# A two-layer graph attention network on one core: layer 1's edge masks made by ScalarE in two operations instead of by one comparison on VectorE

## Chip, cores and metric

The kernel runs on one core of a Trainium2 chip. The metric is the device time of one execution in microseconds (us). Three runs of the kernel before took 2610.62, 2584.36 and 2599.78 us, so the median is 2599.78 us. The other two lie 0.4 and 0.6% from it.

## What is computed

The input is a graph of N = 6250 nodes with 768 features and E = 100000 edges, sorted by destination node. The node features go through a layer norm and a ReLU, then two graph attention layers, then a two-layer perceptron, and the result is added to the input:

```python
h = jnp.maximum(_layernorm(x, axis=-1), 0.0)
x = x + _L0_gnn_ref(h, edge_index, W1, ..., bm2)

def gat_conv(x, src, dst, W, a_src, a_dst, bias, heads):
    h = (x @ W).reshape(n, heads, -1)
    alpha_s = (h * a_src[None]).sum(-1)
    alpha_d = (h * a_dst[None]).sum(-1)
    e = jax.nn.leaky_relu(alpha_s[src] + alpha_d[dst], NEG_SLOPE)
    m = jax.ops.segment_max(e, dst, num_segments=n)
    e = jnp.exp(e - m[dst])
    denom = jax.ops.segment_sum(e, dst, num_segments=n)
    alpha = e / (denom[dst] + 1e-16)
    out = jax.ops.segment_sum(h[src] * alpha[:, :, None], dst, num_segments=n)
    return out.reshape(n, -1) + bias
```

Each node also has an edge to itself. Layer 1 has 4 heads of 64 features, layer 2 one head of 256. The work that matters here is the edge work of layer 1: for each edge, fetch the source node's row, find the weight of the edge from a number of the source and a number of the destination, and add the weighted row to the destination's sum.

## The kernel before

**Tiling.** Nodes are in 49 tiles of 128 (NT). Edges are in tiles of 128; four edge tiles make a group g (196 groups), two groups make a unit u (98 units), and four groups g = 4t to 4t+3 make a period t, which belongs to node tile t because the edges are sorted by destination. The stages follow each other: features of layer 1 (until about 190 us), edges of layer 1 (about 195 to 1420 us), edges of layer 2 with the perceptron (about 1480 us to the end).

**One group of layer 1.** GpSimd (POOL) issues one indirect DMA for each edge tile, which gathers the source rows from the table in DRAM into `G` (line 700), up to 8 groups ahead. VectorE (DVE) compares the destinations with a row of numbers 0 to 127 to make the one-hot matrices `hot` (line 724). It works out the edge weights in lines 781 and 782, multiplies the gathered rows with them into `hw` (line 784), and TensorE (PE) adds them up per destination with `o_ps += hot^T hw` (line 804). VectorE takes finished sums over into `acc` (line 822), ScalarE (ACT) copies their parts into `sum` (line 831).

**The masks.** To give every edge the factor of its destination node, the kernel needs the transposed one-hot matrix, `mask`: the row of destinations (mod 128) of 1024 edges is loaded into all 128 partitions (`drow`, bf16, line 660 on the SP queue), and partition p of the mask is 1 where the destination equals p. One VectorE operation makes the mask of a unit, 128x1024 bf16, in `make_mask` (line 714), with the partition's number p (`pidx_ps`) as second operand. TensorE then multiplies the 16 edge tiles of a period with a table of node factors into `e_parts` (line 747, function `meet`); ScalarE copies the result out as `parts_sb` (line 759, `parts_out`), and VectorE adds its three parts up (line 766, `join`). `parts` has one PSUM buffer, so the next `meet` waits for `parts_sb`. In the loop over g, `make_mask` is called at g = 4t+1 and g = 4t+3 for the `meet` at the start of period t+1, whose factors are used in period t+3. There are 98 masks, six buffers for masks and three for `drow`.

**Finished nodes.** When a tile of sums is complete, a generator (`Node1.steps`) is advanced twice per group and turns it into a row block of layer 2: VectorE lines 1050 to 1068, TensorE transposes into `tp` (line 1010), ScalarE `rT` (line 1016), TensorE `h_ps` (line 1076), ScalarE `kept` and `sd` (lines 1080, 220, 221, 1084), and a store into layer 2's table on the SP queue.

**Missing rows.** 46 gathers of layer 1 were issued before the table was complete. What they lack is added later: VectorE makes `soon_hit` (line 335), TensorE multiplies it with the rows kept on chip (`missing`, line 346, 2 to 20 node tiles each), and VectorE adds the product to `G` (line 353). VectorE executes in order, so behind line 353 stand the weights and `hw` of the same group.

**Order of the work.** The kernel gives every engine its instructions in the order of the Python code; there is no scheduler that would move them. An instruction waits for semaphores of the engines or DMAs whose results it needs, and everything behind it on its engine waits with it.

Of the kernel before, what the change touches and what calls it, by code (L numbers as in the profile page):

```python
# [10 lines left out]
F32 = mybir.dt.float32  # L11
BF16 = mybir.dt.bfloat16
I32 = mybir.dt.int32
AF = mybir.ActivationFunctionType
ALU = mybir.AluOpType
AX = mybir.AxisListType

P = 128
# [9 lines left out]
NT = -(-N // P)  # L28
# [44 lines left out]
def kernel(  # L73
# [21 lines left out]
    nc = tc.nc  # L95
# [3 lines left out]
    def pool(name, bufs, **kw):  # L99
        return ctx.enter_context(tc.tile_pool(name=name, bufs=bufs, **kw))  # L100

    const = pool("const", 1)
# [15 lines left out]
    pidx = const.tile([P, 1], F32, name="pidx")  # L118
# [9 lines left out]
    late_nid = min(SOON_FROM, NEXT_FROM)  # L128
    wide = 4 * (HID // 4 + 1)
# [3 lines left out]
    def part_ps(n):  # L133
        at_ps[0] += n
        return both_ps[:, at_ps[0] - n:at_ps[0]]

    iota_ps, nid_ps, mine_ps, rden_ps, pidx_ps = (part_ps(n) for n in (P, NT - late_nid, wide, 8, 1))
    own_ps = part_ps(4 * P - at_ps[0])
    nc.vector.tensor_copy(iota_ps, iota)
    nc.vector.tensor_copy(nid_ps, nid[:, late_nid:])  # L140
    nc.vector.tensor_copy(pidx_ps, pidx)
    eps_c = const.tile([P, 1], F32, name="eps_c")
    nc.vector.memset(eps_c, EPS)
    idle = const.tile([P, 4 * P], BF16, name="idle")
# [1 line left out]
    ones_c = const.tile([P, 1], F32, name="ones_c")  # L146
# [499 lines left out]
    drow, mask = {}, {}  # L646
# [15 lines left out]
    def layer_edges(layer, H, node, pre, matched, pre_pool):  # L662
# [4 lines left out]
        with tc.tile_pool(name=f"eg{layer}", bufs=6) as eg, \  # L667
# [36 lines left out]
            def both(u):  # L704
                return tiles(2 * u)[0], TPG + tiles(2 * u + 1)[-1] + 1

            def make_mask(u):

                if layer == 2 or not 0 <= u < NU:
                    return  # L710
                a, b = (t * P for t in both(u))
                mask[u] = maskp.tile([P, 8 * P], BF16, name="mask")
                at = u % 2 * 8 * P
                nc.vector.tensor_tensor(mask[u][:, a:b], drow[u // 2][:, at + a:at + b],  # L714
                                        pidx_ps.to_broadcast([P, b - a]), ALU.is_equal)

            def make_hot(g):

# [150 lines left out]
            if layer == 1:  # L869
                fetch_rows(0)  # L870
                soon_away(0)
                for r in range(1, 3):
                    fetch_rows(r)
                soon_sources(pre_pool, 0)
                fetch_rows(3)
                for u in range(4):
                    make_mask(u)
            else:
                next_away()
# [55 lines left out]
            for g in range(NG):  # L935
# [20 lines left out]
                if j == 0:  # L956
                    if layer == 1:
                        fetch_rows(t + 4)
                    node.prefetch(t)
                    if layer == 1:  # L960
                        meet(t + 2 if t > 0 else 1)
                elif j == (2 if t < NT - 1 else 1):
                    node.ahead(t)
                elif j % 2 and (layer == 2 or t > 0):
                    make_mask((g + (11 if layer == 1 else 7)) // 2)
                if layer == 1 and t == 0:
                    for u in ((), (4, 5), (6,), (7,))[j]:
                        make_mask(u)
                    if j == 1:
                        parts_out(1)  # L970
                    if j == 2:
                        meet(2)
# [576 lines left out]
```

## Time and profile before

| what | value |
|---|---|
| median of three runs | 2599.78 us |
| the profiled execution: time, span | 2625.26 us, 2623.5 us |
| mean granted TensorE clock in it | 0.809 of full speed |
| busy: PE, DVE, ACT, POOL | 1760.9, 1544.5, 426.2, 1522.5 us |
| the 98 masks (line 714) on VectorE | 118.1 us together |

The page lists the busy time of each engine, then the span in 40 slices, the DMA queues, the chain of work that ended last, and the costliest groups of instructions with the idle time of their engine just before them and what ended it. `PEld` is the weight load of a matmul. Starts of matmuls are recorded, but their ends are modelled, so an engine that waits for a matmul may start well after the end that is shown. A releaser that the profile could not name is "remote" in the lists of waits and "another core or an unknown queue" in the chain; with one core it is not another core.

### The profile page before, as it was taken

The page shows a single profiled execution, that of the slowest core. Times are in us where ns is not written, and L with a number is a line of the kernel's source. Part 1 is how long each engine was busy: PE and PEld are TensorE (multiplying, and loading weights), DVE is VectorE, ACT ScalarE, POOL GpSimd, SP SyncE. Part 2 cuts the span into 40 slices and gives each one's busy share as a digit, 9 for nine tenths or more (in the row PEclk, how much of TensorE's full clock was granted, in tenths as well). Part 3 has the DMA queues.
Part 4 walks back from the last instruction along what each step waited for, and adds up shares of the span by engine and source line. Part 5 has one row for each costly group of instructions (what it writes and reads, how often), then busy time and mean ns, then how long its engine had stood idle before and what let it go on. Part 6 is the DMA issues. An engine that isn't in the chain of part 4 may idle for free.

```text
span 2623.5 us, 23350 instructions
## 1 busy us (share of the span) xinstructions
PE 1760.9 (67%) x7244; PEld 1321.8 (50%) x7246; DVE 1544.5 (59%) x2880; ACT 426.2 (16%) x1330; POOL 1522.5 (58%) x1666
## 2 busy tenths in 40 slices
PE   9861776767577678677666247777666667666667
PEld 7751555555455456455554135455545455554444
DVE  7633566656655756656656256656556655665565
ACT  6640011111111111111112001111111111111111
POOL 5256655655655655555564656666666666666660
PEclk9985888878788777788777578988788888887789
DMA  9885334444433444444442634444444444444441
GB/s 350 284 252 173 111 107 118 115 114 115 128 114 110 125 118 113 120 114 113 124 111 71 181 81 121 141 118 134 131 123 136 127 128 128 134 133 126 120 130 66
DMA packets 144491, 351.43 MB, mean 134 GB/s; under 512 B 33815, under 2 KB 57454, under 8 KB 144358
## 3 DMA queue, kind: packets, MB, share of 16 engines
q0 software_dynamic: 75040, 210.90, 29.5%
q1 hardware_dynamic: 68092, 137.74, 16.1%
q10 hardware_dynamic: 1226, 1.22, 0.2%
q8 instruction: 59, 0.97, 0.2%
q14 instruction: 74, 0.61, 0.1%
HBM read 308.14 MB, written 41.59 MB: 133 GB/s over the span
## 4 chain that ended last, share of the span: by engine, by line
DVE 30%; PE 27%; another core or an unknown queue 25%; issue 12%; ACT 2%; POOL 2%; DMA 2%; DVEq 1%; SPq 0%; POOLq 0%; ACTq 0%
PE o_ps L804 13%; DVE hot L724 5%; PE missing L346 5%; DVE hw L784 4%; PE h_ps L494 4%; DVE u_ps L797 3%; DVE u_ps L795 3%; DVE mask L714 3%; DVE soon_hit L335 2%; PE y_ps L1204 2%; DVE hot L798 2%; POOL G L700 2%; DVE acc L822 2%; PE missing L404 1%
## 5 line engine op out<-in xcount | busy, mean ns | idle before, releaser
L700 POOL DMA_INDIRECT G<-table,src_i x1498 | 1420.4, 948 | 974.4 <-issue 381.7
L804 PE MATMUL o_ps<-G,hot 128*128 128x258 f32 x1564 | 471.7, 457 | 373.2 <-DVE hot L798 235.9
L804 PE MATMUL o_ps<-hw,hot 128*128 128x260 f32 x1564 | 508.6, 473 | 243.8 <-issue 100.9
L804 PEld LDWEIGHTS o_ps<-G,hot 128*128 128x128 f32 x1564 | 350.6, 230 | 479.8 <-DVE hot L798 258.4
L804 PEld LDWEIGHTS o_ps<-hw,hot 128*128 128x128 f32 x1564 | 354.8, 234 | 356.7 <-issue 128.8
L831 ACT ACTIVATE sum<-acc 32x260 f32<-32x260 f32 (+1 forms) x384 | 160.0, 417 | 1137.3 <-DVE acc L822 549.0
L795 DVE TENSOR_TENSOR u_ps<-rho_ps,G 128x512 f32<-128x512 f32 (+1 forms) x197 | 135.3, 687 | 323.0 <-remote 286.9
L346 PE MATMUL missing<-kept,soon_hit 128*128 128x268 f32 x1028 | 263.6, 407 | 31.0 <-issue 30.2
L724 DVE TENSOR_TENSOR hot<-iota_ps,dcol 128x512 f32<-128x512 f32 x392 | 265.8, 679 | 0.0
L784 DVE TENSOR_TENSOR hw<-G,factors 128x1040 f32<-128x1040 f32 (+1 forms) x198 | 242.2, 1223 | 35.3 <-remote 22.3
L353 DVE SCALAR_TENSOR_TENSOR G<-G,soon_ok,missing 128x268 f32<-128x268 f32 x46 | 22.7, 493 | 385.6 <-remote 219.6
L346 PEld LDWEIGHTS missing<-kept,soon_hit 128*128 128x128 f32 x1028 | 200.7, 198 | 76.8 <-issue 41.2
L1204 PE MATMUL y_ps<-wm,mT 128*128 128x384 f32 x392 | 157.2, 525 | 0.6 <-ACT mT L1199 0.6
L494 PE MATMUL h_ps<-w,r 128*128 128x264 f32 (+1 forms) x588 | 144.1, 400 | 18.2 <-ACT r L484 9.6
L797 DVE TENSOR_TENSOR u_ps<-u_ps,G 128x512 f32<-128x512 f32 (+1 forms) x197 | 136.7, 694 | 6.7
L798 DVE TENSOR_TENSOR hot<-hot,u_ps 128x512 f32<-128x512 f32 (+1 forms) x197 | 134.2, 681 | 6.8
L494 PEld LDWEIGHTS h_ps<-w,r 128*128 128x128 f32 x588 | 112.5, 198 | 40.4 <-ACT r L484 10.5
L714 DVE TENSOR_TENSOR mask<-drow,iota_ps 128x1024 bf16<-128x1024 bf16 x98 | 118.1, 1207 | 13.4 <-DMA drow<-dmod_d 13.4
L1204 PEld LDWEIGHTS y_ps<-wm,mT 128*128 128x128 f32 x392 | 68.2, 194 | 60.9 <-issue 33.7
L311 POOL DMA_INDIRECT G<-table,soon_i x46 | 45.6, 991 | 86.9 <-DMA bT<-in_b 54.3
L1080 ACT ACTIVATE kept<-h_ps 128x256 f32<-128x256 f32 x49 | 18.9, 385 | 461.5 <-remote 334.9
L822 DVE SCALAR_TENSOR_TENSOR acc<-acc,keep,o_ps 128x260 f32<-128x260 f32 (+1 forms) x192 | 91.6, 477 | 1.9 <-PE o_ps L804 1.9
(433 smaller groups left out, 1425.9 us busy)
## 6 DMA issues: line engine op xcount, KB each, us to landing
xt<-in_x SPq DMA_DIRECT2D x96, 384.0 KB
drow<-dmod_d SPq DMA_DIRECT2D x49, 512.0 KB
G<-table,src_i POOLq DMA_INDIRECT x1498
out<-y SPq DMA_DIRECT2D x48, 384.0 KB
xTt<-in_xT SPq DMA_DIRECT2D x41, 384.0 KB
table<-kept SPq DMA_DIRECT2D x49, 134.0 KB
table<-kept SPq DMA_DIRECT2D x49, 129.5 KB
soon_d<-G SPq DMA_DIRECT2D x23, 268.0 KB
```

What stands on the lines that cost most here:

```text
L346: nc.tensor.matmul(soon_p[k], hit[:, T - there], kept[T], start=(T == there), stop=(T == NT - 1))
L494: nc.tensor.matmul(h_ps[:, :n], r[:, k], w1[:, k, :n], start=(k == 0), stop=(k == KI - 1))
L700: nc.gpsimd.indirect_dma_start(out=G[g][:n, t], out_offset=None, in_=table[layer], in_offset=bass.IndirectOffsetOnAxis(ap=src_i[:n, k:k + ...
L714: nc.vector.tensor_tensor(mask[u][:, a:b], drow[u // 2][:, at + a:at + b], pidx_ps.to_broadcast([P, b - a]), ALU.is_equal)
L724: nc.vector.tensor_tensor(hot[g][:, T[0]:T[0] + n], iota_ps.unsqueeze(1).to_broadcast([P, n, P]), dcol[:, k:k + n].unsqueeze(2).to_broadca ...
L784: nc.vector.tensor_mul(hw[:, of], Gg[:, :, :RW[1]].rearrange("p t (h c) -> p t h c", h=H), w.unsqueeze(3).to_broadcast([P, n, H, C + 1]))
L795: nc.vector.tensor_mul(u_ps[:, of], row.unsqueeze(1).to_broadcast([P, n, P]), e2.to_broadcast([P, n, P]))
L797: nc.vector.tensor_max(u_ps[:, of], u_ps[:, of], e1.to_broadcast([P, n, P]))
L798: nc.vector.tensor_mul(hot[g][:, of], hot[g][:, of], u_ps[:, of])
L804: nc.tensor.matmul(o_ps[u], hot[g][:, k], r, start=(g % 2 == 0 and k == 0), stop=(g % 2 == 1 and k == tiles(g)[-1]))
L831: nc.scalar.activation(done[t][r], acc[r], AF.Copy)
L1204: nc.tensor.matmul(y_ps, mT[:, j], wm2[:, j, s * half:(s + 1) * half], start=False, stop=(j == KH - 1))
```

## The change

`make_mask` no longer uses VectorE. ScalarE first writes the absolute difference |d - p| of the destination and the partition's number into the mask (function Abs, with the bias -p from a new constant `less_p`), then overwrites it with max(0, 1 - that) (function Relu, scale -1, bias 1). For whole numbers this is 1 where they are equal and 0 elsewhere, as before. The copy of `pidx` in PSUM goes, and a one-column VectorE operation makes `less_p` in its place.

```diff
-    iota_ps, nid_ps, mine_ps, rden_ps, pidx_ps = (part_ps(n) for n in (P, NT - late_nid, wide, 8, 1))
+    iota_ps, nid_ps, mine_ps, rden_ps = (part_ps(n) for n in (P, NT - late_nid, wide, 8))
     own_ps = part_ps(4 * P - at_ps[0])
     nc.vector.tensor_copy(iota_ps, iota)
     nc.vector.tensor_copy(nid_ps, nid[:, late_nid:])
-    nc.vector.tensor_copy(pidx_ps, pidx)
+    less_p = const.tile([P, 1], F32, name="less_p")
+    nc.vector.tensor_scalar(less_p, pidx, -1.0, None, ALU.mult)
...
                 mask[u] = maskp.tile([P, 8 * P], BF16, name="mask")
                 at = u % 2 * 8 * P
-                nc.vector.tensor_tensor(mask[u][:, a:b], drow[u // 2][:, at + a:at + b],
-                                        pidx_ps.to_broadcast([P, b - a]), ALU.is_equal)
+                nc.scalar.activation(mask[u][:, a:b], drow[u // 2][:, at + a:at + b], AF.Abs,
+                                     bias=less_p)
+                nc.scalar.activation(mask[u][:, a:b], mask[u][:, a:b], AF.Relu, bias=ones_c, scale=-1.0)
```

Line numbers in the changed kernel are one higher up to line 713 and two higher behind the mask.

ScalarE's order in one period of layer 1, before (here and below a name in front of an arrow is what is written):

```order
L1016 ACTIVATE rT<-tp,bT_102 128x128 [waits PE_49,Activation_49]
L1016 ACTIVATE rT<-tp,bT_102 128x128
L831 ACTIVATE sum<-acc 32x260 [waits DVE_49]
L831 ACTIVATE sum<-acc 32x260 [waits Activation_49]
L1080 ACTIVATE kept_135<-h_ps 128x256 [waits PE_49]
L220 ACTIVATE kept_135<-h_ps 128x1
L221 ACTIVATE kept_135<-h_ps 128x1
L1084 ACTIVATE sd_101<-h_ps 128x2
L759 ACTIVATE parts_sb<-e_parts 128x192
```

and in one period now:

```order
L1018 ACTIVATE rT<-tp,bT_103 128x128 [waits PE_49]
L1018 ACTIVATE rT<-tp,bT_103 128x128
L715 ACTIVATE mask<-drow,less_p 128x1024 [waits DMAHW6_49]
L717 ACTIVATE mask<-mask,ones_c 128x1024 [waits Activation_49]
L833 ACTIVATE sum<-acc 32x260 [waits DVE_49]
L833 ACTIVATE sum<-acc 32x260
L1082 ACTIVATE kept_129<-h_ps 128x256 [waits PE_49]
L221 ACTIVATE kept_129<-h_ps 128x1
L222 ACTIVATE kept_129<-h_ps 128x1
L1086 ACTIVATE sd_102<-h_ps 128x2
L715 ACTIVATE mask<-drow,less_p 128x1024
L717 ACTIVATE mask<-mask,ones_c 128x1024 [waits Activation_49]
```

with `parts_sb` right behind. One mask of the period now stands between `rT` and the sums, the other between `sd` and `parts_sb`, that is behind the wait for `h_ps`.

VectorE's order where a mask stood ahead of the weights of the next group, before:

```order
L724 TENSOR_TENSOR hot<-iota_ps,dcol 128x512
L714 TENSOR_TENSOR mask<-drow,iota_ps 128x1024
L335 TENSOR_TENSOR soon_hit<-soon_of,iota_ps 128x256
L781 TENSOR_TENSOR factors<-G,factors 128x4x4
L782 TENSOR_TENSOR factors<-factors,G 128x4x4
L784 TENSOR_TENSOR hw<-G,factors 128x1040
```

and now:

```order
L726 TENSOR_TENSOR hot<-iota_ps,dcol 128x512
L336 TENSOR_TENSOR soon_hit<-soon_of,iota_ps 128x256
L783 TENSOR_TENSOR factors<-G,factors 128x4x4
L784 TENSOR_TENSOR factors<-factors,G 128x4x4
L786 TENSOR_TENSOR hw<-G,factors 128x1040
```

Only the mask is gone; `hw` moves up by one operation (the second operand of the mask, `pidx_ps`, lay in the same PSUM tile as `iota_ps` and is shown under that name).

VectorE's order where a mask stood right ahead of the addition of the missing rows, before:

```order
L724 TENSOR_TENSOR hot<-iota_ps,dcol 128x512
L714 TENSOR_TENSOR mask<-drow,iota_ps 128x1024
L353 SCALAR_TENSOR_TENSOR G<-G,soon_ok,missing_6893 128x268
L335 TENSOR_TENSOR soon_hit<-soon_of,iota_ps 128x1792
L781 TENSOR_TENSOR factors<-G,factors 128x4x4
```

and now:

```order
L726 TENSOR_TENSOR hot<-iota_ps,dcol 128x512
L354 SCALAR_TENSOR_TENSOR G<-G,soon_ok,missing_7248 128x268
L336 TENSOR_TENSOR soon_hit<-soon_of,iota_ps 128x1664
L783 TENSOR_TENSOR factors<-G,factors 128x4x4
L784 TENSOR_TENSOR factors<-factors,G 128x4x4
```

VectorE comes to its wait for `missing` one operation earlier. TensorE's, GpSimd's and SP's orders keep their instructions; ScalarE loads its function tables once in both kernels.

## The prediction

> **What bounds the kernel now.** I read the busy times and the chain on the page first, then layer 1's share of them by windows (columns PE, PEld, DVE, ACT, POOL, granted clock, DMA share, GB/s), because only layer 1 has masks.
>
> ```profile
> PE 1760.9 (67%) x7244; PEld 1321.8 (50%) x7246; DVE 1544.5 (59%) x2880; ACT 426.2 (16%) x1330; POOL 1522.5 (58%) x1666
> DVE 30%; PE 27%; another core or an unknown queue 25%; issue 12%; ACT 2%; POOL 2%; DMA 2%; DVEq 1%; SPq 0%; POOLq 0%; ACTq 0%
> ```
>
> ```profile
> 195.00:1420.00 1225.00, 827.78 (x3639) 631.44 (x3640) 739.11 (x1374) 145.78 (x517) 689.74 (x729) 0.79 0.42 117
> ```
>
> No engine is full: in layer 1's 1225 us TensorE is busy 828, VectorE 739, GpSimd 690 and ScalarE 146. The chain alternates between VectorE and TensorE, with a quarter that waits for something unnamed. So I asked what these two wait for inside layer 1.
>
> ```profile
> L714 DVE TENSOR_TENSOR mask<-drow,iota_ps 128x1024 bf16<-128x1024 bf16 x97 | 117.1, 1210 | 13.4 <-DMA drow<-dmod_d 13.4
> ...
> L353 DVE SCALAR_TENSOR_TENSOR G<-G,soon_ok,missing 128x268 f32<-128x268 f32 x46 | 22.7, 493 | 385.6 <-remote 219.6 <-PE o_ps L804 80.2 <-PE missing L346 63.5
> ```
>
> ```profile
> PE o_ps L804 <- DVE hw L784: 95.4, 40, 6.8
> PE o_ps L804 <- DVE kept L1082: 45.5, 20, 4.5
> ```
>
> VectorE's idle time, 1225 - 739 = 486 us, has one main place: 385.6 us stand before line 353, which waits for TensorE's product `missing`, 8.4 us each time. In turn TensorE waits 95.4 + 45.5 = 141 us for VectorE's `hw` (line 1082 only happens to end with `hw`). The two engines take turns: while TensorE works off `missing`, VectorE stands at line 353; when it is released it must make weights and `hw`, and TensorE runs dry. Work on VectorE counts only if it lies between the release and an `hw` that TensorE already waits for. The masks' 118 us are therefore not the gain.
>
> **The change, part by part.** *Removed: 98 comparisons on VectorE*, 1.21 us each. For each one in the timeline I asked what follows it on VectorE, and whether TensorE stood idle until that. Four of them fall into about 50 us, and they are of three kinds. The first and the last of the first kind:
>
> ```profile
> 300.87 1.21 DVE L714 TENSOR_TENSOR mask<-drow,iota_ps 128x1024 bf16<-128x1024 bf16 x1
> ...
> 306.44 0.80 PE L804 MATMUL o_ps<-hw,hot 128*128 128x260 f32 x1 [3.20 <-DVE hw L784]
> ```
>
> ```profile
> 1351.90 1.21 DVE L714 TENSOR_TENSOR mask<-drow,iota_ps 128x1024 bf16<-128x1024 bf16 x1
> ...
> 1355.60 0.71 PE L804 MATMUL o_ps<-hw,hot 128*128 128x260 f32 x2 [2.08 <-issue]
> ```
>
> The mask stands ahead of an `hw`, and TensorE, idle for 3.20 and 2.08 us, begins as soon as that `hw` is there. There are 22 such masks from 300 to 1352 us, each worth its whole 1.21 us, and one pair at 230 us worth 1.5: 22 x 1.21 + 1.5 = 28.1 us. The other two kinds:
>
> ```profile
> 661.70 1.21 DVE L714 TENSOR_TENSOR mask<-drow,iota_ps 128x1024 bf16<-128x1024 bf16 x1
> ...
> 665.77 3.23 PE L804 MATMUL o_ps<-hw,hot 128*128 128x260 f32 x14
> ...
> 669.28 1.21 DVE L714 TENSOR_TENSOR mask<-drow,iota_ps 128x1024 bf16<-128x1024 bf16 x1
> 681.44 0.49 DVE L353 SCALAR_TENSOR_TENSOR G<-G,soon_ok,missing 128x268 f32<-128x268 f32 x1 [10.95 <-remote]
> ```
>
> Behind the mask at 661.70 TensorE is busy without a gap when the `hw` comes; there are 46 of that kind or nearly so. The one at 669.28 is the last work before line 353, which then stands for 10.95 us; there are 26 of that kind. I cost both at nothing: what covers them is TensorE's own work and the wait for `missing`, which was issued before them. If that cover were gone they would be worth up to 72 x 1.21 = 87 us more.
>
> *Added: 196 operations on ScalarE.* No row has Abs or this Relu on 128x1024; the nearest are these.
>
> ```profile
> L449 ACT ACTIVATE logv<-mv,eps_c 128x1 f32<-128x1 f32 x49 | 13.8, 282 | 7.5 <-DVE mv L447 7.5
> ...
> L451 ACT ACTIVATE rstd<-logv 128x1 f32<-128x1 f32 x49 | 9.9, 203 | 1.6
> ...
> L257 ACT ACTIVATE drm<-dri 98x1024 bf16<-98x1024 int32 x1 | 1.0, 1040 | 0.0
> ```
>
> 1024 elements took 1040 ns without a bias column; a bias column makes 282 of 203, 79 ns more. So one operation takes 1.12 us and the dependent pair 2.24, at least 2.08 (no charge for the bias) and about 2.4 with a gap for the wait between them. That is 98 x 2.24 = 220 us on an engine with 146 of 1225 us busy: it has room, and only its place in the order can hurt. The Trainium skill (ScalarE: Activation LUTs, What ACT_TABLE_LOAD costs) gives 280 ns + 0.833 ns per element with a bias column; by it, an estimate, the operation takes 1.13 us, which agrees.
>
> *Moved: the wait of TensorE for the masks.* The second mask of a period now stands on ScalarE between `kept`, which waits for `h_ps`, and `parts_sb`; behind that stand the next sums and `rT`. `meet` needs both the mask and the bank that `parts_sb` frees. First and last period, and a bad one between:
>
> ```profile
> 351.32 0.36 ACT L759 ACTIVATE parts_sb<-e_parts 128x192 f32<-128x192 f32 x1
> ...
> 360.32 0.62 PE L747 MATMUL e_parts<-win,mask 128*128 128x12 bf16 x16
> ```
>
> ```profile
> 709.50 0.32 PE L747 MATMUL e_parts<-win,mask 128*128 128x12 bf16 x7 [1.95 <-ACT parts_sb L759]
> ```
>
> ```profile
> 1379.15 0.36 ACT L759 ACTIVATE parts_sb<-e_parts 128x192 f32<-128x192 f32 x1
> ...
> 1385.46 0.57 PE L747 MATMUL e_parts<-win,mask 128*128 128x12 bf16 x14
> ```
>
> From the end of `parts_sb` to `meet` there are 8.6 us in the first case and 5.9 in the last; in the middle one TensorE stood for 1.95 us until `parts_sb`. Of the 43 such hand-overs with `kept` in front, 39 have 5.3 us or more and hide 2.24 us. Three (at 412, 617 and 709 us) have none and pay it in full, 3 x 2.24 = 6.7 us; the one at 804 us has 2.5. The first mask of a period, behind `rT`, is followed by a `kept` that waits anyway for `h_ps`, 10 us a time. `drow` is fetched a period ahead, and the SP queue's next fetch waits for masks two periods old: no cost.
>
> *The start of layer 1.* Masks 2 and 3 wait for their `drow`, and with them VectorE's whole queue, in which the copy (line 187) stands that frees `parts` for the first `meet`:
>
> ```profile
> 194.89 2.35 DVE L714 TENSOR_TENSOR mask<-drow,iota_ps 128x1024 bf16<-128x1024 bf16 x2 [5.46 <-DMA drow<-dmod_d]
> ...
> 205.15 2.35 DVE L714 TENSOR_TENSOR mask<-drow,iota_ps 128x1024 bf16<-128x1024 bf16 x2 [7.91 <-DMA drow<-dmod_d]
> ...
> 208.23 0.59 PE L747 MATMUL e_parts<-win,mask 128*128 128x12 bf16 x16 [13.76 <-issue]
> ...
> 226.93 0.33 ACT L759 ACTIVATE parts_sb<-e_parts 128x192 f32<-128x192 f32 x1 [39.09 <-issue]
> ```
>
> Now that copy no longer stands behind them, masks 0 and 1 on ScalarE end near 194.9 + 2 x 2.24 = 199.4, and the first `meet` begins there, 8.8 us earlier. `parts_sb` stands behind masks 2 and 3, which end at 205.15 + 4.5 = 209.6, well before 226.93. If the unexplained 18 us from `meet` to `parts_sb` stay as long, 8.8 us are gained; if they end at a fixed time, nothing; 17 at most. I take 8.8, since the wait is one for `meet`'s own result.
>
> *Sum:* -28.1 + 6.7 - 8.8 = -30 us. The constant `less_p` takes the place of a copy of the same size, cost nothing. The profiled execution took 2625.3 us (span 2623.5 and 1.8 around it), so it would take 2595; it is 25.5 us above the median of the runs, and 2599.8 - 30 gives 2570.
>
> **Rivals.** *A: the masks weigh what the chain says.* The chain's shares within layer 1 (200 to 1400 us):
>
> ```profile
> by line: another core or an unknown queue 22.9%; issue 15.6%; PE o_ps L804 11.7%; PE missing L346 11.2%; DVE hw L784 9.2%; DVE hot L724 5.7%; DVE mask L714 5.5%; DVE soon_hit L335 4.9%; POOL G L700 2.0%; DVE factors L782 2.0%; DVE acc L822
> ```
>
> 5.5% of 1200 us is 66 us, which gives 2534. For it: gaps of TensorE that shrink may also keep its clock up (0.79 granted here). Against: where the chain meets an unnamed releaser it goes on to the instruction before on the same engine, so it counts masks like the one at 669.28, which a stall follows. The Trainium skill (TensorE: Matmul & The Clock Gate, What's actually happening) says that the array's clock falls to half after an idle window of about 3.4 us and comes back after a busy one; shorter gaps would then speed up the matmuls behind them.
>
> *B: TensorE is late anyway.* The 14 matmuls behind `missing` are recorded from 665.77 on, yet line 353, which needs only `missing`, starts at 681.44. If TensorE's results come that late because it works off more than its recorded times show, VectorE gets ready earlier only to stand longer, and the 22 gaps were no gaps: -8.8 + 6.7, about -2, 2598. Against it: in the 22 gaps TensorE starts at once when `hw` is there, as an engine with nothing left to do would.
>
> *C: ScalarE's order becomes the bound, and the kernel slower.* If `kept` comes later or `meet` earlier than now, so that mask and `parts_sb` are late in most periods, TensorE's queue stops at `meet` with every `o_ps` behind it: 43 x 2.24 = 96 us more and 37 (28.1 + 8.8) less, +59, 2659. It decides once 37 / 2.24 = 17 periods pay in full. Against it: 39 of 43 have 5.3 us, and VectorE saves only 1.2 us of a path per two periods. The Trainium skill speaks for this side (ScalarE: Activation LUTs, Rules for kernel authors): it wants `relu`, `max` and the like on VectorE, which is up to about three times as fast. Here the pair would take 2.24 us against 1.21; that matters only if the masks lie on the path on ScalarE.
>
> That the change does not do what it says I rule out: the order shows the masks gone from VectorE, and no added load of function tables on ScalarE.
>
> **How the numbers follow.** Forecast 0.42, A 0.22, B 0.22, C 0.14. A change of about 1%, 26 us, is what a measurement of this kernel can tell from none. The forecast's own range, -45 to -10 (with the start at 17 or 0, the masks of the second kind worth a few us), lies beyond -26 in 0.6 of cases: 0.25. With A, faster is 0.47. Same is the rest of the forecast (0.17), B (0.22) and a mild C (0.04): 0.43. Slower is 0.10. The range goes from 2505, past A with the clock's part, to 2620, the near end of C; 0.15 or so is left out.
>
> **What would show it.** In the new profile VectorE's busy time is 118 us lower and ScalarE's 220 higher; each operation of the pair takes 1.0 to 1.2 us; the idle time before line 353's successor (now 354) grows by about 30 us, the 26 masks ahead of it; TensorE's wait for `hw`, 141 us, falls by about 28; TensorE waits for `parts_sb` or masks in few periods; the first `meet` starts near 200 us. I am wrong if layer 1 shrinks by over 60 us (A), if TensorE's waits fall and layer 1 stays (B), or if TensorE waits for ScalarE at `meet` in 17 periods or more (C).

## The result, and the profile after

The changed kernel takes 2584.5 us, the kernel before 2597.8 us (medians of 20 runs each): a ratio of 0.9943, interval 0.9927 to 0.9960, so 13.3 us less (10 to 19). The direction is the one forecast, the size less than half of the 30 us.

The two profiled executions lie further apart than that: spans 2623.5 and 2591.9 us, 31.6 us. The profiled execution of before took 15 us more than the slowest of its 20 runs; the one of after is the slowest of its 20. So 18 of the 31.6 us are chance, and a difference between these two profiles has to be taken with that in mind.

The page of the changed kernel, its layer 1 by windows (columns PE, PEld, DVE, ACT, POOL, granted clock, DMA share, GB/s), and groups of that window:

```profile
PE 1757.1 (68%) x7245; PEld 1323.4 (51%) x7246; DVE 1432.8 (55%) x2782; ACT 639.4 (25%) x1526; POOL 1517.5 (59%) x1666
```

```profile
195.00:1420.00 1225.00, 824.17 (x3648) 631.56 (x3648) 635.40 (x1296) 357.45 (x721) 700.08 (x741) 0.80 0.42 117
```

```profile
L715 ACT ACTIVATE mask<-drow,less_p 128x1024 bf16<-128x1024 bf16 x96 | 110.7, 1153 | 6.0 <-DMA drow<-dmod_d 6.0
L717 ACT ACTIVATE mask<-mask,ones_c 128x1024 bf16<-128x1024 bf16 x96 | 110.0, 1146 | 3.1
...
L354 DVE SCALAR_TENSOR_TENSOR G<-G,soon_ok,missing 128x268 f32<-128x268 f32 x46 | 22.7, 493 | 445.2 <-remote 224.0 <-PE missing L347 98.4 <-PE o_ps L806 85.7
```

The work moved as forecast: VectorE is 112 us less busy over the execution, ScalarE 213 us more, and the two operations take 1.15 us each. But VectorE's idle time ahead of the addition of the missing rows (line 354, formerly 353) is 445.2 us where it was 385.6: 60 us more, twice what I expected. What TensorE waits for, in the same window:

```profile
PE o_ps L806 <- DVE hw L786: 75.3, 36, 12.1
PE missing L347 <- issue: 70.0, 66, 2.3
PE e_parts L749 <- ACT parts_sb L761: 61.4, 4, 26.9
PE o_ps L806 <- DVE kept L1084: 51.7, 21, 4.2
```

The wait for `hw` (first and last line together) is 127.0 us where it was 141: 14 us less, not 28. The wait for `parts_sb` grew from 25.2 us in 2 places to 61.4 in 4. Idle time ahead of `missing` that the profile puts down to nothing ("issue") more than doubled. Before, these two were

```profile
PE missing L346 <- issue: 30.2, 34, 2.3
PE e_parts L747 <- ACT parts_sb L759: 25.2, 2, 23.3
```

### The profile page after: what moved, and what is told of

It reads as the page before. It is cut to its first block, busy times and chain, and to the rows that moved or that the text cites. A ratio compares the mean times of both kernels' runs of the same rounds, so it can differ in the third digit from the quotient of the medians.

```text
span 2591.9 us, 23416 instructions
## 1 busy us (share of the span) xinstructions
PE 1757.1 (68%) x7245; PEld 1323.4 (51%) x7246; DVE 1432.8 (55%) x2782; ACT 639.4 (25%) x1526; POOL 1517.5 (59%) x1666
## 4 chain that ended last, share of the span: by engine, by line
PE 33%; DVE 23%; another core or an unknown queue 23%; issue 13%; ACT 3%; DMA 2%; POOL 2%; DVEq 1%; SPq 0%; ACTq 0%; POOLq 0%
PE o_ps L806 15%; PE missing L347 7%; DVE hot L726 4%; PE h_ps L495 4%; DVE hw L786 4%; DVE u_ps L799 3%; DVE u_ps L797 3%; PE missing L405 2%; DVE soon_hit L336 2%; DVE hot L800 2%; PE y_ps L1206 2%; DVE acc L824 1%; DMA G<-table,src_i 1%; PE h_ps L1078 1%
## 5 line engine op out<-in xcount | busy, mean ns | idle before, releaser
L806 PE MATMUL o_ps<-hw,hot 128*128 128x260 f32 x1564 | 498.6, 468 | 208.8 <-issue 80.0
L354 DVE SCALAR_TENSOR_TENSOR G<-G,soon_ok,missing 128x268 f32<-128x268 f32 x46 | 22.7, 493 | 445.2 <-remote 224.0
L1082 ACT ACTIVATE kept<-h_ps 128x256 f32<-128x256 f32 x49 | 18.8, 384 | 515.8 <-remote 371.9
L1201 ACT ACTIVATE mT<-tp,bm1c 128x128 f32<-128x128 f32 x98 | 30.5, 362 | 356.9 <-PE o_ps L806 179.0
L715 ACT ACTIVATE mask<-drow,less_p 128x1024 bf16<-128x1024 bf16 x98 | 112.9, 1152 | 12.9 <-issue 6.9
L717 ACT ACTIVATE mask<-mask,ones_c 128x1024 bf16<-128x1024 bf16 x98 | 112.3, 1146 | 3.2
```

The lines of the kernel that those rows point to most:

```text
L715: nc.scalar.activation(mask[u][:, a:b], drow[u // 2][:, at + a:at + b], AF.Abs, bias=less_p)
L806: nc.tensor.matmul(o_ps[u], hot[g][:, k], r, start=(g % 2 == 0 and k == 0), stop=(g % 2 == 1 and k == tiles(g)[-1]))
```

## Experiments

All of them came from chips that behave differently from that of the prediction, so the first two runs matter most. The record numbers these chips 1 (e1 to e4), 10 (e5 to e10) and 3 (e11 and e12); the kernel before took 2087 to 2093 us on each of them. Below, the first chip is that of the prediction's runs, and the other chip stands for these three. Ratios are against the kernel before, run beside them on the same chip.

### The same two kernels elsewhere (e1, e2)

No edit.

> The kernel before, unchanged, profiled a second time. The two profiles at hand differ by 31.6 us of span, the medians by 13.3. If the first profile of the kernel before was merely a long execution, this one comes near 2598 us and is shorter by some 25 us, and the place where it is shorter tells which part of the 31.6 us was chance. If profiles of this kernel always take that long, it is again near 2625.

> The changed kernel, unchanged, profiled a second time: near 2585 us, 9 us below its first profile. With the second profile of the kernel before it shows by stage where the 13 us of the medians lie: the forecast puts 8.8 in the start of layer 1 (up to 205 us) and 21 in its steady part, 0 in layer 2.

Measured: 2091.4 and 2090.7 us, one run each; the kernel before had a median of 2091.8 in 23 runs beside them. Neither expectation holds. Whether the first chip is one of these three in another condition, the runs do not say. Layer 1 of the kernel before there, the group of line 353 and that of the gathers in the same window:

```profile
195.00:1094.00 899.00, 731.55 (x3622) 593.15 (x3620) 737.58 (x1377) 144.77 (x529) 679.96 (x720) 0.91 0.56 153
```

```profile
L700 POOL DMA_INDIRECT G<-table,src_i x711 | 672.3, 946 | 216.6 <-issue 182.2 <-DMA G<-table,src_i 9.1 <-DVE o L1068 4.9
L353 DVE SCALAR_TENSOR_TENSOR G<-G,soon_ok,missing 128x268 f32<-128x268 f32 x46 | 22.5, 489 | 37.4 <-PE missing L346 37.3
```

One gather takes 946 ns, as on the first chip (948). What is gone is the waiting for TensorE: 37.4 us before line 353 instead of 385.6, released by `missing` itself and no longer by something unnamed. Now GpSimd sets the pace: of the 216.6 us between its gathers, 182.2 are time in which it waits for nothing that the profile shows, 0.26 us a gather; the waits listed next take 9.1 and 4.9 us. On the first chip 535.0 us lay between the gathers of layer 1, with waits for VectorE in the first place:

```profile
L700 POOL DMA_INDIRECT G<-table,src_i x727 | 689.1, 948 | 535.0 <-DVE hw L784 205.6 <-issue 189.8 <-DVE kept L1082 73.3
```

VectorE and TensorE have time to spare, and the change is worth nothing: most of what VectorE saves goes into longer waits for the gathers ahead of the weights, in e1 and in e2

```profile
DVE factors L781 <- DMA G<-table,src_i: 59.1, 49, 3.1
```

```profile
DVE factors L783 <- DMA G<-table,src_i: 133.5, 82, 4.8
```

Counted as in the prediction, e1 has 23 masks of the first kind (7, 11, 15 and so on to 95): TensorE stands idle for 1.0 to 5.1 us and begins as soon as the `hw` behind the mask is there. With all masks off VectorE (e2) they are worth nothing here, and so they are when they alone are moved (e4, below); that count alone does not give a price.

### Masks left out, a quarter of them, and both engines (e3 to e6)

The edit of e3 and e5 (masks 6 and later are left out, and earlier ones used in their place):

```
+                if u > 5:
+                    mask[u] = held[u % 4 + 1]
+                    return
-                mask[u] = maskp.tile([P, 8 * P], BF16, name="mask")
+                mask[u] = held[u] = maskp.tile([P, 8 * P], BF16, name="mask")
```

That of e4 puts `if u % 4 == 3 and u > 3:` ahead of ScalarE's pair and keeps the comparison on VectorE for the rest; that of e6 is the kernel before and in addition the pair into a scratch tile:

```
+                spare = maskp.tile([P, 8 * P], BF16, name="spare", bufs=1)
+                nc.scalar.activation(spare[:, a:b], drow[u // 2][:, at + a:at + b], AF.Abs,
+                                     bias=less_p)
+                nc.scalar.activation(spare[:, a:b], spare[:, a:b], AF.Relu, bias=ones_c, scale=-1.0)
```

> Masks 0 to 5 are made on ScalarE as in the change; all later ones are left out and earlier masks are used again, so neither engine has that work (the output is wrong). Theory 1, the shortfall against the forecast is ScalarE's order (masks late for meet, kept or parts_sb late behind masks): without ScalarE's part the whole price on VectorE is seen, -35 us or more against the kernel before (28.1 of the direct ones and up to 8.8 of the start). Theory 2, VectorE's freed time goes into longer waits for TensorE at line 354: as the change, -13 us, at most -18. Rival A of the prediction: -66 us.

> Only masks 7, 11, 15, ... (every fourth, those that stood directly ahead of an hw for which TensorE was idle; 23 of 98) are made on ScalarE; the others stay on VectorE. Forecast: it has the 22 direct masks and no start, -27 us and at most two late hand-overs back, -25. Theory 2 (freed time goes into longer waits for TensorE): -7 us or less. Theory 1 (ScalarE's order costs some 15 us in the change): a quarter of that cost, -27 + 4 = -23.

> The kernel without the later masks (e3) once more, because the runs of e1 to e4 came from a chip that is granted a clock of 0.91 and needs 2091 us for the kernel before, not the 2598 us and 0.81 of the prediction's runs. There every variant took the same time, since the gathers on GpSimd set the pace and line 353 stood for 37 us in all. If these runs are granted 0.8 or so and the kernel before takes near 2600: by ScalarE's order as the cause of the shortfall -35 us or more; by the freed time of VectorE going into longer waits for TensorE as the change, -13, at most -18. If they are granted 0.91: again no difference, within 3 us.

> The kernel before, its masks made on VectorE as ever, and beside that the pair of ScalarE's operations for each mask into a scratch tile that nobody reads: ScalarE's order alone, without the relief of VectorE and without TensorE's wait for a mask from ScalarE. At a clock near 0.8: by the forecast 3 late hand-overs, +7 us; by ScalarE's order as the cause of the shortfall +15 to +20; by the waits for TensorE as the cause, 0 to +5. At 0.91: 0, within 3 us.

Measured: e3 2092.7 us, ratio 1.0000 (0.9990 to 1.0010); e4 2091.7, 1.0001 (0.9991 to 1.0012); e5 2091.6, 0.9995 (0.9985 to 1.0006); e6 2093.1, 1.0000 (0.9991 to 1.0009). Where the gathers are the bound, 118 us of VectorE's work can go and 220 us can be put on ScalarE, and nothing changes. In e4 VectorE's wait for gathers ahead of the weights is 84.5 us, 25 more than in e1, close to the 23 x 1.21 = 27.8 us that its masks took. That tells no theory of the first chip from another; only the part of e5 and e6 on a clock of 0.91 came true.

### TensorE made late (e7 to e10)

So I made TensorE late on the other chip, with work that can be seen. In the kernel before (e7), the change (e8), the kernel without later masks (e9) and that with a quarter of the masks on ScalarE (e10), every `missing` is computed twice:

```
-            for T in range(there, NT):
+            for T in [*range(there, NT)] * 2:
                 nc.tensor.matmul(soon_p[k], hit[:, T - there], kept[T], start=(T == there),
                                  stop=(T == NT - 1))
```

> The chip of e1 to e6 does not have what the prediction's runs had: TensorE's results long after the recorded matmuls. This kernel brings it about: the kernel before, with every product missing computed twice over (the second pass starts the accumulation anew, so the result is the same). That is some 22 matmuls of 0.26 us ahead of each line 353, 5.8 us x 46 = 267 us of TensorE work. Layer 1 then has more TensorE work than time (487 of 600 us busy before, some 650 after), so this takes 2190 to 2360 us, and VectorE's idle time before line 353 rises from 37 us to over 250. It is the base for e8 to e10.

> The change, with every product missing computed twice. Against e7: if the shortfall of the change comes from a late TensorE (freed time of VectorE goes into longer waits at line 354), 5 to 15 us less. If the direct count holds, -30. If the change is worth nothing as soon as TensorE is the bound (rival B in full), within 3 us.

> Masks 6 and later left out on both engines (as in e3), with every product missing computed twice. Against e8: if ScalarE's order costs something in the change (masks, kept and parts_sb late), at least 10 us less than e8; if it costs nothing, within 4 us of e8.

> Only masks 7, 11, 15, ... on ScalarE (as in e4), with every product missing computed twice. By the direct count these 23 masks have the whole gain of the steady part, so it comes within 4 us of e8, less what the start brings. If which mask is exposed depends on where TensorE stands, a quarter to a half of e8's gain.

| run | median us | ratio to the kernel before | against e7 |
|---|---|---|---|
| e7, masks on VectorE | 2195.9 | 1.0521 (1.0506 to 1.0536) | |
| e8, masks on ScalarE | 2148.8 | 1.0298 (1.0284 to 1.0312) | -47.1 |
| e9, no later masks | 2147.3 | 1.0289 (1.0275 to 1.0304) | -48.6 |
| e10, a quarter on ScalarE | 2167.5 | 1.0388 (1.0368 to 1.0407) | -28.4 |

Layer 1 of e7 from its first to its last `hw`, and two of its waits (from 195 us on):

```profile
186.68:1200.64 1013.96, 917.51 (x4649) 764.93 (x4650) 737.73 (x1381) 143.89 (x523) 683.80 (x724) 0.97 0.50 137
```

```profile
DVE G L353 <- PE missing L346: 240.9, 34, 13.3
...
PE o_ps L804 <- DVE hw L784: 91.4, 58, 4.7
```

The same of e8:

```profile
186.47:1149.08 962.61, 902.87 (x4650) 756.37 (x4651) 632.04 (x1287) 348.15 (x711) 683.31 (x723) 0.99 0.53 144
```

```profile
DVE G L354 <- PE missing L347: 295.2, 38, 14.4
...
PE o_ps L806 <- DVE hw L786: 55.0, 56, 3.9
```

e7 is within its range, with 241 us before line 353 where over 250 were expected. Here is the mechanism of the prediction, and it pays more than forecast. Layer 1 shrinks by 51 us: 37 are TensorE's idle time, nearly all of it the wait for `hw`, and 15 are TensorE's own busy time (918 to 903), with the clock at 0.99 for 0.97. VectorE's idle time at line 353 grows by 54 us all the same; time may be lost there while the path gets shorter.

What ScalarE's order costs is e8 against e9, of which the medians differ by 1.6 us. First and last `hw` of layer 1 in e8:

```profile
186.47 1.24 DVE L786 TENSOR_TENSOR hw<-G,factors 128x1040 f32<-128x1040 f32 x1
...
1148.39 0.69 DVE L786 TENSOR_TENSOR hw<-G,factors 128x520 f32<-128x520 f32 x1
```

and in e9:

```profile
189.83 1.24 DVE L789 TENSOR_TENSOR hw<-G,factors 128x1040 f32<-128x1040 f32 x1
...
1151.49 0.69 DVE L789 TENSOR_TENSOR hw<-G,factors 128x520 f32<-128x520 f32 x1
```

e9 begins 3.4 us later and ends 3.1 us later: over some 960 us, ScalarE's pairs cost 0.3 us in these two executions. That is less than the runs of one kernel differ among themselves (3 to 5 us here), so no cost is seen. And e10: its 23 masks, the places where I had counted (the count finds the same 23 in e7), give 28.4 us, 1.23 each. That looks like their whole length on VectorE, but it is the sum of two things. Layer 1 of e10 from first to last `hw`:

```profile
186.03:1170.22 984.19, 907.72 (x4651) 759.60 (x4652) 711.84 (x1358) 193.43 (x569) 684.54 (x725) 0.99 0.51 141
```

It is 29.8 us shorter than in e7; 20.0 of that are TensorE's idle time, 0.87 a mask, and 9.8 its own busy time at a higher clock, which the count left out. The other 75 masks give 19 us more, 0.25 each, the start and the clock included. None of my three expectations for e8 had 47 us; of those for e9 and e10, "costs nothing" is right, and a quarter of the masks has 60% of the gain, between the two answers I had written down.

### TensorE made later still (e11, e12)

The same edit with `* 3`.

> The kernel before with every product missing computed three times over: another 237 us of TensorE work (half of the 474 us that missing takes in e7). Layer 1 of e7 had 91.5 us in which TensorE waited for hw, so little of it finds room: 2380 to 2430 us, and TensorE's wait for hw shrinks to 40 to 70 us, since the longer product gives VectorE time to get ahead.

> The change with every product missing computed three times over, against e11. If a TensorE that is late with recorded work is enough to explain why the prediction's chip gave 13 us and not 30, the gain sinks from e8's 47 us to 5 to 20 us, as TensorE becomes the bound (rival B on its way to nothing). If what counts is the path from line 353 to the next hw, which is the same after every stall however long the product took, the gain stays at 25 us or more, and the prediction's chip must have lost its 15 us in another way.

Measured: 2416.9 us, ratio 1.1577 (1.1559 to 1.1596), and 2374.1, 1.1370 (1.1353 to 1.1387): the change is worth 42.7 us. TensorE's wait for `hw` in e11 and in e12:

```profile
PE o_ps L804 <- DVE hw L784: 78.7, 56, 3.8
```

```profile
PE o_ps L806 <- DVE hw L786: 53.2, 56, 3.0
```

The time of e11 lies where it was expected; its wait for `hw`, expected at 40 to 70 us, is above. Its third pass, 221 us of time over e7, took only 13 of the 91 us of this wait and left the gain of the change at 43 us, the second of the two answers written down for e12. That fits a gain that lies in the stretch from line 353 to the next `hw`, which comes after each stall however long it lasted. Rival B, TensorE late with work of its own, does not make the change worthless.

## Why the prediction was right or wrong

**The start of layer 1 failed: forecast -8.8 us, measured no gain, +1.5 in e8 against e7 and +2.7 in the two profiles.** The prediction took 8.8 "since the wait is one for `meet`'s own result". In e7 the first `meet` and the first `hw` are

```profile
184.40 0.59 PE L747 MATMUL e_parts<-win,mask 128*128 128x12 bf16 x16 [13.23 <-DVE w L187]
```

```profile
186.68 1.24 DVE L784 TENSOR_TENSOR hw<-G,factors 128x1040 f32<-128x1040 f32 x1
```

and in e8, on TensorE and then on ScalarE:

```profile
172.02 0.38 PE L749 MATMUL e_parts<-win,mask 128*128 128x12 bf16 x8 [2.54 <-ACT mask L717]
```

```profile
180.39 1.15 ACT L715 ACTIVATE mask<-drow,less_p 128x1024 bf16<-128x1024 bf16 x1 [6.21 <-DMA drow<-dmod_d]
...
184.84 0.31 ACT L761 ACTIVATE parts_sb<-e_parts 128x192 f32<-128x192 f32 x1
```

`meet` begins 12.4 us earlier, but the first `hw` only 0.2 us (186.68 to 186.47, above). Counted from the start of `aps`, a product ahead of any mask, it even comes 1.5 us later; in e7 and in e8 that is

```profile
169.32 1.84 PE L193 MATMUL aps<-w2a,w2T 128*128 128x2 f32 x8 [16.20 <-DMA w2T<-in_W2T]
```

```profile
167.65 1.84 PE L194 MATMUL aps<-w2a,w2T 128*128 128x2 f32 x8 [14.90 <-DMA w2T<-in_W2T]
```

`parts_sb` stands on ScalarE behind masks 2 and 3, and these wait for their `drow`. The wait that VectorE's queue lost went into ScalarE's, ahead of the next thing on the path. I had seen that order and set it aside, because on the first chip `parts_sb` came late for another reason. There the start went like this, before:

```profile
192.64 1.84 PE L193 MATMUL aps<-w2a,w2T 128*128 128x2 f32 x8 [15.78 <-DMA w2T<-in_W2T]
```

```profile
259.20 0.33 ACT L759 ACTIVATE parts_sb<-e_parts 128x192 f32<-128x192 f32 x1 [31.94 <-remote]
260.20 0.33 ACT L759 ACTIVATE parts_sb<-e_parts 128x192 f32<-128x192 f32 x1 [0.66 <-PE e_parts L747]
```

and after:

```profile
185.74 1.84 PE L194 MATMUL aps<-w2a,w2T 128*128 128x2 f32 x8 [16.58 <-DMA w2T<-in_W2T]
```

```profile
189.42 0.38 PE L749 MATMUL e_parts<-win,mask 128*128 128x12 bf16 x8 [1.83 <-issue]
...
216.37 0.33 ACT L761 ACTIVATE parts_sb<-e_parts 128x192 f32<-128x192 f32 x1 [14.29 <-remote]
...
251.36 0.33 ACT L761 ACTIVATE parts_sb<-e_parts 128x192 f32<-128x192 f32 x1 [30.23 <-remote]
251.59 1.14 ACT L715 ACTIVATE mask<-drow,less_p 128x1024 bf16<-128x1024 bf16 x1
...
256.03 0.31 ACT L761 ACTIVATE parts_sb<-e_parts 128x192 f32<-128x192 f32 x1
```

The product `aps` happens to start 6.9 us earlier in the profile after, when its weights land. The first `meet` came earlier as forecast, and by more: 11.9 us beyond those 6.9. But from there to the first `parts_sb`, which the prediction kept at 18 us, it now took 27.0 (189.42 to 216.37), so only 3.7 us were left of it there. By the third `parts_sb` only 4.2 us of that are left (260.20 to 256.03): two masks, 4.6 us on ScalarE, stand between the second and the third, where 0.66 us of waiting stood. So the start lost 2.7 us.

**The rest of the sum, -28.1 + 6.7, came out near, in part by luck, for its terms did not come out.** From the third `parts_sb` to the last `hw` of layer 1 the windows are, before and after:

```profile
260.20:1425.90 1165.70, 823.80 (x3587) 628.13 (x3588) 723.35 (x1360) 147.38 (x523) 652.13 (x688) 0.80 0.41 113
```

```profile
256.00:1400.60 1144.60, 808.97 (x3580) 619.91 (x3580) 618.75 (x1263) 343.12 (x704) 649.27 (x687) 0.81 0.42 116
```

21.1 us less; the sum without its start and without the pair at 230 us was -26.6 + 6.7 = -19.9. Yet TensorE's idle time, 342 and 336 us, fell by 6 only, and its busy time by 15. With the start's +2.7, layer 1 gained 18.4 us between these two executions, of which 5 must be chance if the medians' 13.3 are right and all of the change's effect lies there; the 6.9 us before and 6.3 us in layer 2, where nothing was changed, are the rest of the 18. The direct count itself is borne out in part, in e10: 20.0 us of TensorE's idle time where 23 x 1.21 = 27.8 were counted, and 9.8 us of its busy time that were not. (Of the masks right ahead of line 353 the trace has 23, numbers 9, 13 and so on to 97, and not 26; costed at nothing, they move no term.)

**The hand-overs: forecast three, found five.** The three of the prediction are there (410, 607 and 702 us), and two more at 800 and 900. ScalarE and TensorE at one of them:

```profile
699.15 0.38 ACT L1082 ACTIVATE kept<-h_ps 128x256 f32<-128x256 f32 x1 [20.51 <-remote]
...
701.84 0.31 ACT L761 ACTIVATE parts_sb<-e_parts 128x192 f32<-128x192 f32 x1
```

```profile
680.20 1.04 PE L1078 MATMUL h_ps<-w,rT 128*128 128x258 f32 x4
...
690.45 3.71 PE L806 MATMUL o_ps<-hw,hot 128*128 128x260 f32 x8 [3.83 <-issue]
702.20 0.60 PE L749 MATMUL e_parts<-win,mask 128*128 128x12 bf16 x7 [8.04 <-issue]
```

The mask's 2.3 us stand between `kept` and `parts_sb` as the prediction said, and TensorE begins as `parts_sb` ends. Five times 2.3 is 11.5 us where 6.7 were forecast. With the start and the hand-overs as measured, the sum is -28.1 + 2.7 + 11.5 = -13.9 us, close to the 13.3 of the medians; the next paragraph shows why that is no proof. On the other chip there is no such place after the start, which is e9's answer: the price needs a `kept` that comes late.

**Why TensorE's wait for `hw` fell by 14 and not by 28** stays open in part. By place, between the third `parts_sb` and the last `hw`, TensorE's idle time fell by 34.6 us ahead of `o_ps` (239.5 to 204.9) and by 37.7 ahead of the transposes `tp` (43.8 to 6.1). It grew by 39.8 ahead of `missing` (30.2 to 70.0, above) and by 26.9 ahead of `meet` (25.2 to 52.1). So the gaps that the prediction counted did shrink, and nearly as much idle time came up in two other places; of that, the pairs explain 11.5 us at `meet`. At the five late hand-overs VectorE waits too. Its waits ahead of `hw`, before and after, and one of them:

```profile
DVE hw L784 <- remote: 22.3, 5, 8.0
```

```profile
DVE hw L786 <- remote: 46.7, 7, 10.1
...
703.42 1.24 DVE L786 TENSOR_TENSOR hw<-G,factors 128x1040 f32<-128x1040 f32 x1 [9.02 <-remote]
```

In the program this `hw` waits for its weights, which VectorE itself has just made, and for its buffer, which TensorE's `o_ps` of an earlier group gives back. By the records TensorE had been idle from 694.2 us on; `kept`, too, started at 699.15, 18 us after the recorded end of `h_ps` at 681.2. Nor is that one case: in layer 1 on the first chip, ScalarE's waits ahead of `kept` that are put down to "remote" are 327.2 us in 27 places before and 371.9 in 24 after; in e1 there is none. By these figures TensorE's results come long after its recorded matmuls on the first chip. That VectorE, ready earlier, then waits for them is rival B in part; these waits fit it, and no run tests it. e11 and e12 show that being late with recorded work does not do this. What else holds TensorE up there was not found, since no experiment ran on that chip.

**The rivals.** *A* (-66 us) did not come about, but its second half did: as the gaps shrank, TensorE's own work got quicker, 15 of e8's 51 us. *B* holds in part, as above; the wholly hidden case exists, with GpSimd in TensorE's place (e1 to e6). *C* did not come about: it needs 17 late periods, and the first chip had five; on the other chip e8 against e9 shows no cost. Its rule in the Trainium skill (ScalarE: Activation LUTs, Rules for kernel authors), to keep `relu` and the like on VectorE, goes by the price of an operation and says nothing on the path. The price agrees for the pair (2.30 us on ScalarE, 1.21 on VectorE), though not for one operation of it (1.15 us), and no run here has a `relu` on VectorE. On the path, the cheaper engine was the wrong place.

## What to carry to other kernels

An operation that moves to an engine with room takes its waits along: at the new place, look at what stands behind it in the queue before you book the wait as gone (here `parts_sb` behind two masks that wait for a DMA). Count a removed operation only where the next engine stands idle for what follows it, but do not take that count for the price: the same 23 masks gave 20 us of TensorE's idle time and 8 us besides where TensorE and VectorE took turns (e10), and nothing where GpSimd was the bound (e4), since VectorE then waited for the gathers instead. So ask as well what the relieved engine will wait for next. Two profiles of one kernel can differ by more than the change, so compare stages that the change cannot touch before reading a difference as an effect.

## What the runs showed that was not expected

- The same program took 2598 us in the prediction's runs and 2092 in the experiments. The durations of single operations agree (a gather 948 and 946 ns, a mask 1.21 us on both); the difference lies with TensorE: in layer 1 it is busy for 828 us at a clock of 0.79 against 732 at 0.91, and the waits for it are longer, above all 385.6 us against 37.4 before line 353. A wait that the profile puts down to "remote" for 20 us, behind a matmul that by the record is over, was the sign of it. The Trainium skill (TensorE: Matmul & The Clock Gate, Seeing it yourself) warns that records of the clock can be unreliable and that a clock stuck at a quarter for over 50 us has been seen; results 18 us late would fit that, and no run here shows it.
- More work raised TensorE's granted clock: 0.91 in layer 1 of e1, where it was busy 732 of 899 us, and 0.97 in e7, busy 918 of 1014. The Trainium skill (TensorE: Matmul & The Clock Gate, What's actually happening) has idle time lower the clock and activity restore it; this agrees.
